# Both w transforms of a spectral layer as four 64x64 tiles, with the residual kept on chip in rows split by parity

## The chip, the cores and the metric

The kernel runs on one core of one Trainium2 chip. The metric is the device time of one execution in microseconds. The kernel before takes 3664.48 us, the median of 3 runs (3661.27 to 3665.77).

## The reference

The input x has shape (2, 48, 48, 768): two images of 48 by 48 tokens and 768 channels, all in f32. Two layers follow each other, both with a residual:

```
x = x + attention(group_norm(x))        # 12 heads of 64, relative positions in h and w, then proj_w, proj_b
x = x + spectral(group_norm(x))

spectral(v):
    f = rfft2(v, axes=(h, w), norm="ortho")           # 48 x 25 complex per channel
    o1 = gelu(complex block matmul(f, w1) + b1)       # 8 blocks of 96 channels
    o2 = softshrink(complex block matmul(o1, w2) + b2, 0.01)
    return irfft2(o2, s=(48, 48), norm="ortho")
```

The change concerns the end of the first layer (projection and residual) and the two one-dimensional transforms over w in the second: the forward one at the beginning, the inverse one at the end.

## The kernel before, in words

**Stages.** The attention of both images comes first. Then, for each image b, `project_out` (L887) multiplies the attention's output by proj_w, adds it to x, and takes the transform over w; `Spectral` (L952) does the rest of layer 1. While one stage ends, steps of the next projection are run ahead of time: `Projection.fill` and `step` (L811 to L818) are called from attention and from `prepare` in `block_kernel` (L1270).

**The order of the work.** The kernel is written in Bass and Tile; a pool of tiles hands out memory and inserts the waits. Instructions through `InOrder` (L60) stay on their engine in the order in which the program issues them; its line, L68, is the one that the profile gives them. Each engine works through its queue in order. SP (SyncE) issues nearly all DMAs. A DMA of the program takes one of eight completion semaphores in turn, so that it waits for the one eight before it.

**Attention's last steps.** `finish` (L553) copies the output of a unit (18 units for each pair of heads; three share one `res` tile) and stores each full `res` to `oT` in DRAM; `inverses` (L571) transposes the reciprocal denominators on PE (`ps_i`), copies them (`turned`) and stores them to `inv_d` with three DMAs, one for each of three columns x. The last of these end attention.

**The projection.** NT = 18 token tiles of 128 tokens, each in two channel halves of UQ = 384 columns. `Projection.tokens` (L859) loads, for a group g of three token tiles, `oT` and the reciprocals and multiplies them on POOL. `Projection.product` (L843) accumulates six matmuls, 128x128 by 128x384, into a PSUM bank `acc`. PSUM has eight banks, of which this part uses seven.

`project_out` keeps x, and then x1 = x + attention, in six tiles `x2` of 96 rows (two image rows of 48 tokens) by XP = 4 row pairs by 768 channels. `rows(i)` (L900) loads one of them, and POOL adds the bias proj_b to it in four instructions. For each product, `shifts` (L746) cuts the 128 tokens into pieces that lie on aligned partitions, 3 for each token tile, and DVE adds them into `x2` (L941). When four image rows are complete, and one more token tile is under way, `over_w(g)` (L912) transforms them: four matmuls with `fw` (96 rows by 112 columns, block diagonal for two image rows), each over 384 columns, into banks `ps_y`, four copies by ACT (L927) into `y1`, and one store of `y1` by SP to `y_d`, 112 rows. There are 12 such over_w in an image. After the last token tile the over_w still left are done by channel halves.

**The spectral layer.** It goes through four sections s of SC = 192 channels (two blocks n each). `load` (L1079) reads `y_d` into `y2` in five pieces; `over_h` (L1089) transforms over h (`ps_z`); `mean`, `norm`, `first` and `second` (L1040 to L1186) do the group norm and the MLP; `back_h` (L1188) transforms back over h and stores `u_d`. `back_w(s, more)` (L1204) does for one section the inverse transform over w and the residual: for each of the six tiles of `x2`, two matmuls with `iw` (100 rows by 96 columns, 384 columns of `u2`) into `ps_x`, two DVE adds into `x2` (L1221), the fetch of the next section's `u2` (100 rows by 4 row pairs), and the store of the section's channels to `out`. `run` (L1233) calls it with the fetches of the next section one section ahead, and at the end `prepare(True)` and a last `back_w`.

**Between the two images.** In the last section of image A, `prepare` gets the second image's projection ready: memory, weights, the first tokens and the first multiply. The fourier constants `fh`, `fw`, `ih`, `iw`, `gmean` are loaded anew for each image, after `rows(0)`.

Of the kernel before, what the change touches and what calls it, by code (L numbers as in the profile page):

```python
# [17 lines left out]
P = 128  # L18
# [24 lines left out]
YP = 112  # L43
# [232 lines left out]
def attention(tc, k, xs, a, oTs, inv_ds, late, span, ps_b, ps_o):  # L276
# [12 lines left out]
    with ExitStack() as ctx:  # L289
# [63 lines left out]
        by_act, by_dve = [], []  # L353

# [197 lines left out]

        def finish(un):  # L553

            pr, g, x = un["pr"], un["g"], un["x"]
            if x == 0:
                outs[pr, g] = outp.tile([P, 8, 3, 16], F32, tag="res", name="res")
                if g % 3 == 0:
                    dens[pr, g // 3] = outp.tile([P, 3, 2, 3], F32, tag="dens", name="dens")
            res = outs[pr, g]  # L560
            act.copy(res[:, :, x, :], un["o"][:, :P].rearrange("p (y d) -> p y d", d=16))
            dve.tensor_reduce(
                dens[pr, g // 3][:, x, :, g % 3], un["parts"], AX.X, ALU.add
            )
            if x == 2:
                sync.dma_start(
                    out=oTs[pr // NP][pr % NP * P : (pr % NP + 1) * P, g * UQ : (g + 1) * UQ],
                    in_=res.rearrange("p y x d -> p (y x d)"),
                )

        def inverses(pr, half):  # L571
# [12 lines left out]
            def send():  # L584
                dst = inv_ds[pr // NP][pr % NP, half].rearrange("h g (y x d) -> x (h g) y d", x=3, d=16)
                for x in range(3):
                    sync.dma_start(
                        out=dst[x],
                        in_=turned[6 * x : 6 * x + 6, :].rearrange("p (y d) -> p y d", d=16),
                    )  # L590
# [3 lines left out]
        pairs = NP * xs.shape[0]  # L594
# [151 lines left out]
def shifts(t):  # L746


    size = {0: P, 32: 32, 64: 64, 96: 32}
    p = 0  # L750
    while p < P:
        hp, q = divmod(t * P + p, 2 * HW)
        n = min(P - p, 2 * HW - q, size[p], size[q])
        yield p, hp, q, n
        p += n


class Projection:
# [27 lines left out]
    def cut(self, whole, i):  # L786

        return whole[:, self.head + i * NCC * UQ :][:, : NCC * UQ]
# [10 lines left out]
    def w(self):  # L799
        return self.fixed()[:, : NCC * C].rearrange("p (cc f) -> p cc f", f=C)  # L800

    @property
    def pb(self):
        return self.fixed()[:, NCC * C : self.head]
# [82 lines left out]
def project_out(tc, k, x_b, pr, pools, y_d, x2, constants):  # L887
# [9 lines left out]
    R = 2 * HW  # L897
    x_v = x_b.rearrange("(t p) c -> p t c", p=R)

    def rows(i):  # L900

        part = x2[i]
        pr.sync.dma_start(out=part, in_=x_v[:, i * XP : (i + 1) * XP, :])
        for j in range(XP):
            pr.pool.tensor_tensor(part[:, j, :], part[:, j, :], pr.pb[:R], ALU.add)

# [3 lines left out]
    row = lambda hp: x2[hp // XP][:, hp % XP, :]  # L910

    def over_w(g, steps=range(C // SC)):  # L912

        y1 = work.tile([YP, 2, C], F32, tag="y1", name="y1")
        part = x2[2 * g // XP]
        t0 = 2 * g % XP
        for s in steps:
            ch = slice(s * SC, (s + 1) * SC)
            ps = bank("ps_y")
            nc.tensor.matmul(  # L920
                ps[:YP, : 2 * SC],
                lhsT=k.fw,
                rhs=part[:, t0 : t0 + 2, ch],
                start=True,
                stop=True,
            )
            nc.scalar.copy(y1[:, :, ch], ps[:YP, : 2 * SC].rearrange("p (t c) -> p t c", c=SC))  # L927
        ch = slice(steps[0] * SC, (steps[-1] + 1) * SC)
        pr.sync.dma_start(out=y_d[:, 2 * g : 2 * g + 2, ch], in_=y1[:, :, ch])

    turned = 0
    for t in range(NT):
        if t % 3 == 0 and 0 < t < NT - 3:
            pr.tokens(t // 3 + 1)
            rows(t // 3 + 1)
        for hf in range(2):
            cols = slice(hf * UQ, (hf + 1) * UQ)
            acc = pr.product(t, hf)
            for p, hp, q, n in shifts(t):
                dst = row(hp)[q : q + n, cols]  # L940
                nc.vector.tensor_tensor(dst, acc[p : p + n, :UQ], dst, ALU.add)  # L941
            if t == NT - 1:
                half = C // SC // 2
                for g in range(turned, HW // 4):
                    over_w(g, range(hf * half, (hf + 1) * half))
        while t < NT - 1 and (turned + 1) * 2 * R <= (t - 1) * P:
            over_w(turned)
            turned += 1
# [3 lines left out]
class Spectral:  # L952
# [12 lines left out]
    def __init__(self, tc, k, a, pools, x2, y_d, out_b, prepare):  # L965
        self.tc, self.nc, self.k, self.a, self.prepare = tc, tc.nc, k, a, prepare
        self.sync = InOrder(tc, tc.nc.sync)
        self.span, self.ps_b, self.small, self.wp, self.yp, self.up, self.dp, zp = pools
        self.x2, self.y_d = x2, y_d
        self.out_v = out_b.rearrange("(t p) c -> p t c", p=2 * HW)  # L970
# [21 lines left out]
        self.y2, self.u2, self.w, self.power = {}, {}, {}, {}  # L992

# [56 lines left out]
    def norm(self, n):  # L1050
# [24 lines left out]
        for f0 in range(0, NF, 400):  # L1075
            fs = slice(f0, f0 + 400)
            nc.gpsimd.tensor_tensor(self.both[n % 2][:, fs], zf[:, 0, fs], zf[:, 1, fs], ALU.add)

    def load(self, s, pieces):  # L1079

        src = self.y_d[: 4 * KW, :, s * SC : (s + 1) * SC].rearrange(
# [7 lines left out]
    def over_h(self, n):  # L1089
# [7 lines left out]
        for j in range(KW // WP):  # L1097
# [13 lines left out]
            if n == 1 and j == 1:  # L1111
                self.mean(0)
            if n == 1 and j == 3:
# [30 lines left out]
    def second(self, n, ahead):  # L1144
# [9 lines left out]
        for j in range(KW // WP):  # L1154
# [22 lines left out]
            nc.gpsimd.tensor_tensor(val, val, clip, ALU.subtract)  # L1177
# [25 lines left out]

    def back_w(self, s, more):  # L1204


        nc, k = self.nc, self.k
        ch = slice(s * SC, (s + 1) * SC)
        u_d = self.u_d.rearrange("w (q t) c -> (w q) t c", q=4)
        for i, part in enumerate(self.x2):  # L1210
            for t in range(0, XP, 2) if s >= 0 else ():
                ps = self.bank("ps_x")
                nc.tensor.matmul(  # L1213
                    ps[: 2 * HW, : 2 * SC],
                    lhsT=k.iw,
                    rhs=self.u2[s, i][:, t : t + 2, :],
                    start=True,
                    stop=True,
                )
                dst = part[:, t : t + 2, ch]  # L1220
                nc.vector.tensor_tensor(  # L1221
                    dst, ps[: 2 * HW, : 2 * SC].rearrange("p (t c) -> p t c", c=SC), dst, ALU.add
                )
            if more:
                u2 = self.up.tile([4 * KW, XP, SC], F32, tag="u2", name="u2")
                self.sync.dma_start(out=u2, in_=u_d[:, i * XP : (i + 1) * XP, :])
                self.u2[s + 1, i] = u2
            if s >= 0:
                self.sync.dma_start(
                    out=self.out_v[:, i * XP : (i + 1) * XP, ch], in_=part[:, :, ch]  # L1230
                )
# [38 lines left out]
def block_kernel(tc, a, out):  # L1270
    nc = tc.nc
    B = a["x"].shape[0]
    with ExitStack() as ctx:
# [21 lines left out]
        for b in range(B):  # L1295
            oTs.append(dram.tile([C, S], F32, tag=f"oT{b}", name=f"oT{b}"))
            y_ds.append(dram.tile([YP, HW // 2, C], F32, tag=f"y_d{b}", name=f"y_d{b}"))
# [13 lines left out]
        def prepare(rest):  # L1311
# [9 lines left out]
            while rest and ready[-1].steps:  # L1321
                ready[-1].step()

        attention(tc, k, a["x"], a, oTs, inv_ds, late, span, ps_b, ps_o)
        for b in range(B):
            with ExitStack() as ctx2:
# [3 lines left out]
                x2 = [  # L1330
                    pool(f"x2_{i}", 1).tile([2 * HW, XP, C], F32, tag="x2", name=f"x2_{i}")
                    for i in range(HW // 2 // XP)
                ]
# [113 lines left out]
```

## Time and profile before

The profiled execution took 3660.19 us and its span is 3658.4 us; the runs shown have a median of 3664.48 us. PE's granted clock has a mean of 0.987. All times in the table are of that execution, in us from the start of the span.

| what | value |
|---|---|
| time of the profiled execution | 3660.19 us |
| span | 3658.4 us |
| PE busy | 3548.6 us (97%) |
| DVE, ACT, POOL busy | 79%, 70%, 56% |
| attention of both images | 0 to 2838 |
| projection and forward w transform, image A | 2838 to 2988 |
| rest of layer 1, image A | 2988 to 3236 |
| projection and forward w transform, image B | 3236 to 3406 |
| rest of layer 1, image B | 3406 to 3658 |
| ps_y (L920) | 192 records on PE, 66.8 us busy after 2838 |
| ps_x (L1213) | 192 records on PE, 66.7 us busy |
| adds of the product on DVE (L941) | 216, 553 ns each |
| adds of the inverse transform on DVE (L1221) | 96, 553 ns each |
| copies of ps_y on ACT (L927) | 96, 479 ns each |

How to read it: PE is the TensorE's matmuls, PEld its weight loads. An f32 matmul leaves two records (two passes), so a count of records is twice the count of matmuls. DVE is VectorE, ACT ScalarE, POOL GpSimd; SPq is SyncE's queue, where a DMA is issued. `out<-in` names the tiles written and read. The chain of waits is followed back from the last instruction: at each step to what released it. Idle time of an engine that is not the bottleneck costs nothing.

### The profile page before, as it was taken

Reading aid. Unit: us, or ns where it says so; the run is one execution under the profiler, and the core shown is the slowest. Engines: PE = TensorE matmul, PEld = TensorE weight load, DVE = VectorE, ACT = ScalarE, POOL = GpSimd, SP = SyncE. Lnnn points to the kernel's source line nnn. Section 1 sums busy time; section 2 is a strip of 40 time slices with the busy share of each in tenths; the row PEclk is TensorE's granted clock in tenths of the full one; section 3 lists DMA queues with packets and bytes.
Section 4 is the critical chain, followed back from the end, with each engine's and each line's share of the span. In section 5 each row is a group of like instructions: output and inputs, shape, how many; then the busy total and the mean of one; then the engine's idle time right before and its main releaser. Section 6 shows DMA issues by size and latency. Waiting matters only on the chain.

```text
span 3658.4 us, 92606 instructions
## 1 busy us (share of the span) xinstructions
PE 3548.6 (97%) x36032; PEld 2477.2 (68%) x36032; DVE 2902.1 (79%) x6771; ACT 2557.2 (70%) x3769; POOL 2047.2 (56%) x662
## 2 busy tenths in 40 slices
PE   7999999999999999999999999999988999999898
PEld 5677676767767666677676767767666557655675
DVE  4798989989989996799898989899996437743576
ACT  3788888888888888688888888888885124301342
POOL 2567666757575763567666666666673524343232
PEclk9999999999999999999999999999999989999999
DMA  3687778777777885677777777777888743585434
GB/s 105 142 181 171 180 171 179 172 179 171 181 169 175 214 200 122 140 178 174 176 176 171 177 173 175 176 176 172 188 190 190 200 127 85 169 213 147 109 110 140
DMA packets 496484, 607.61 MB, mean 166 GB/s; under 512 B 179117, under 2 KB 311597, under 8 KB 496046
## 3 DMA queue, kind: packets, MB, share of 16 engines
q1 hardware_dynamic: 496046, 601.68, 69.3%
q8 instruction: 286, 4.69, 0.6%
q14 instruction: 152, 1.25, 0.1%
HBM read 131.60 MB, written 87.67 MB: 60 GB/s over the span
## 4 chain that ended last, share of the span: by engine, by line
PE 84%; DVE 5%; ACT 3%; DMA 3%; issue 2%; POOL 1%; SPq 1%; POOLq 0%; DVEq 0%; ACTq 0%
PE ps_o L68 22%; PE ps_s L68 21%; PE ps_proj L68 15%; PE ps_v L68 8%; PE acc L68 7%; DVE s L68 2%; PE ps_u L1195 2%; PE ps L1160 2%; PE ps_y L920 2%; PE ps_r L68 2%; SPq L68 1%; PE ps_x L1213 1%; DMA pT<-s 1%; ACT spectrum L1035 1%; POOL s L68 1%
## 5 line engine op out<-in xcount | busy, mean ns | idle before, releaser
L68 POOL TENSOR_TENSOR s<-rhw 128x2304 f32<-128x2304 f32 x432 | 1740.8, 4062 | 1025.3 <-DMA pT<-s 546.8
L68 DVE CUSTOM_DVE_ANT_0 s<-ps_s,s 128x512 f32<-128x512 f32 (+1 forms) x2160 | 1222.2, 633 | 299.7 <-issue 196.1
L68 ACT ACTIVATE s<-s,nm 128x1152 f32<-128x1152 f32 x864 | 1074.7, 1245 | 335.3 <-DVE nm L68 333.1
L68 DVE STREAM_TRANSPOSE s<-s 128x1152 f32<-128x1152 f32 x864 | 1112.0, 1344 | 6.8 <-ACT s L68 6.8
L68 ACT COPY pT<-s 32x1152 f32<-32x1152 f32 x864 | 993.6, 1150 | 25.9 <-PE ps_o L68 7.5
L68 PE MATMUL ps_o<-pT,v 128*64 128x128 f32 x15552 | 906.5, 276 | 41.7 <-ACT res L68 18.9
L68 PEld LDWEIGHTS ps_o<-pT,v 128*64 128x64 f32 x15552 | 875.4, 139 | 84.0 <-issue 43.6
L68 PE MATMUL ps_s<-kT,qT 64*128 64x512 f32 (+1 forms) x4320 | 899.8, 554 | 4.9 <-DVE mx L68 1.7
L68 PEld LDWEIGHTS ps_s<-kT,qT 64*128 64x128 f32 x4320 | 432.3, 186 | 418.1 <-issue 347.0
L68 PE MATMUL ps_proj<-xnT,w 128*64 128x384 f32 (+1 forms) x4032 | 591.3, 446 | 4.9 <-ACT xnT L68 3.7
L68 PEld LDWEIGHTS ps_proj<-xnT,w 128*64 128x64 f32 x4032 | 281.0, 137 | 278.8 <-issue 212.1
L941 DVE TENSOR_TENSOR x<-acc,x 32x384 f32<-32x384 f32 (+2 forms) x216 | 119.2, 553 | 227.8 <-PE acc L68 163.8
L68 PE MATMUL ps_v<-w,xnT 128*64 128x128 f32 x5184 | 297.3, 274 | 0.0
L68 PEld LDWEIGHTS ps_v<-w,xnT 128*64 128x64 f32 x5184 | 281.7, 137 | 21.2 <-DVE mx L68 21.2
L927 ACT COPY y<-ps_y 112x384 f32<-112x384 f32 x96 | 46.0, 479 | 299.5 <-PE ps_y L920 282.7
L68 DVE DVE_READ_ACCUMULATOR2_ANT mx<- 128x1 f32 x2160 | 179.7, 83 | 0.0
L68 ACT ACTIVATION_READ_ACCUMULATOR s<-s,nm 128x1 f32 x864 | 161.4, 187 | 0.0
L1177 POOL TENSOR_TENSOR spectrum<-spectrum 128x480 f32<-128x480 f32 x80 | 96.3, 1204 | 113.2 <-DVE spectrum L1176 85.0
L1160 PE MATMUL ps<-w,spectrum 96*64 96x96 f32 x3200 | 143.1, 248 | 0.0
L1160 PEld LDWEIGHTS ps<-w,spectrum 96*64 96x64 f32 x3200 | 133.6, 137 | 11.1 <-issue 4.4
L68 PE MATMUL acc<-proj_s 128*128 128x384 f32 x360 | 118.2, 486 | 0.4 <-POOL x L68 0.4
L68 PEld LDWEIGHTS acc<-proj_s 128*128 128x128 f32 x360 | 68.3, 190 | 48.2 <-POOL x L68 0.6
(139 smaller groups left out, 2299.8 us busy)
## 6 DMA issues: line engine op xcount, KB each, us to landing
pT<-s SPq DMA_DIRECT2D x2592, 144.0 KB
t<-rel SPq DMA_DIRECT2D x144, 189.0 KB
rhw<-t SPq DMA_DIRECT2D x144, 144.0 KB
y<-y_d SPq DMA_DIRECT2D x40, 360.0 KB
u_d<-spectrum SPq DMA_DIRECT2D x40, 360.0 KB
u<-u_d SPq DMA_DIRECT2D x48, 300.0 KB
w<-in_qkv_w SPq DMA_DIRECT2D x36, 384.0 KB
oT<-res SPq DMA_DIRECT2D x72, 192.0 KB
```

What stands on the lines that cost most here:

```text
L68: return lambda *args, **kw: self.tc.keep_in_program_order(op(*args, **kw))
L920: nc.tensor.matmul(ps[:YP, : 2 * SC], lhsT=k.fw, rhs=part[:, t0 : t0 + 2, ch], start=True, stop=True,)
L927: nc.scalar.copy(y1[:, :, ch], ps[:YP, : 2 * SC].rearrange("p (t c) -> p t c", c=SC))
L941: nc.vector.tensor_tensor(dst, acc[p : p + n, :UQ], dst, ALU.add)
L1035: self.nc.scalar.activation(junk, part, AF.Square, accum_out=total)
L1160: nc.tensor.matmul(ps[64 * r : 64 * r + 64, w * BS : (w + 1) * BS], lhsT=self.o1[:, ri, f0 : f0 + 64], rhs=w2[:, (0, 2, 1, 0)[2 * r + ri], ...
L1177: nc.gpsimd.tensor_tensor(val, val, clip, ALU.subtract)
L1195: nc.tensor.matmul(ps[: 2 * HW, :480], lhsT=k.ih, rhs=d2[:, c0 : c0 + 480], start=True, stop=True)
L1213: nc.tensor.matmul(ps[: 2 * HW, : 2 * SC], lhsT=k.iw, rhs=self.u2[s, i][:, t : t + 2, :], start=True, stop=True,)
```

## The change

In words:

- The residual is one tile `x1` of 128 partitions by 24 row pairs by 768 channels, held over both images and put at a place that attention's memory occupied. Even image rows lie on partitions 0 to 47, odd ones on 64 to 95 and 112 to 127 (tokens 0 to 31 and 32 to 47 of the row). Partitions 48 to 63 and 96 to 111 are filled with other rows and meet zeros in `fw`. A group of rows is loaded by four or five DMAs (it was one), and `moves` cuts a token tile into 3, 5 and 5 pieces for the adds (it was 3 each).
- `over_w` uses `fw` as 64x64 tiles: for each channel half four matmuls, one for each combination of two row groups and two column groups, into two banks, with one ACT copy for each bank. `y1` is stored by two DMAs of 50 rows, issued by ACT.
- over_w(2g) stands right after token tile 3g+2, and over_w(2g-1) after token tile 3g: one token tile sooner than before. The last three token tiles go by channel halves: all of half 0, then all of half 1, with the over_w in between.
- `back_w` uses `iw` in the same way: 24 matmuls of 50 rows by 64 columns instead of 12 of 100 by 96. `u2` is fetched by two DMAs of 50 rows. The stores to `out` are three for each three groups of rows (18 in the last section), and the fetches are no longer each followed by a store.
- In attention `inv_d` is stored by five DMAs instead of three, in an order that makes parities contiguous; for the last unit these and the store of `oT` are issued by ACT.
- `prepare` also runs two products (`fill(2)`) for the second image before its `back_w`. The fourier constants are loaded once. `mean(0)` and `norm(0)` come one piece of over_h sooner. The pool of `y2` has 10 buffers (it had 8). POOL's instructions of the spectral layer go through `InOrder`.

```diff
 def finish(un):  def send():
+        def queue(pr, g):
+            return act if (pr, g) == (pairs - 1, HW // 8 - 1) else sync
...
                 for x in range(3):
-                    sync.dma_start(
-                        out=dst[x],
-                        in_=turned[6 * x : 6 * x + 6, :].rearrange("p (y d) -> p y d", d=16),
-                    )
+                    src = turned[6 * x : 6 * x + 6, :].rearrange("p (k i d) -> p k i d", i=2, d=16)
+                    if x == 2:
+                        to.dma_start(
+                            out=dst[:, :, 1, :], in_=src.rearrange("p k i d -> p k (i d)")
+                        )
+                        continue
+                    for i in range(2):
+                        to.dma_start(
+                            out=dst[:, :, 2 * i, 16 * x : 16 * x + 16], in_=src[:, :, i, :]
+                        )
...
+def moves(t):
+    done = 0
+    for p in range(0, P, 32):
+        k, m = divmod(t % 3 * 4 + p // 32, 3)
+        if p >= done:
+            n = min(P, p + 96 - 32 * m) - p if p in (0, 64) and m == 0 else 32
+            yield p, n, k, 32 * m
+            done = p + n
+        if m == 1:
+            yield p, 32, k, 96
...
+    def rows(g):
+        part = x1[:, 4 * g : 4 * g + 4, :]
+        pr.sync.dma_start(out=part[:HW], in_=x_v[g, 0])
+        pr.sync.dma_start(out=part[64:96], in_=x_v[g, 1, :32])
+        for i in range(2):
+            pr.sync.dma_start(out=part[96 + 16 * i : 112 + 16 * i], in_=x_v[g, i, 32:])
+        if pr.room is None:
+            pr.sync.dma_start(out=part[HW:64], in_=x_v[g, 1, 32:])
+        for j in range(4):
+            pr.pool.tensor_tensor(part[:, j, :], part[:, j, :], pr.pb, ALU.add)
...
+    def over_w(n, halves=range(2)):
+        y1 = work.tile([P, 2, C], F32, tag="y1", name="y1")
+        for hf in halves:
+            cols = slice(hf * UQ, (hf + 1) * UQ)
+            both = [bank(f"ps_y{i}") for i in range(2)]
+            for c in range(2):
+                for i in range(2):
+                    r = slice(64 * i, 64 * i + 64)
+                    pr.pe.matmul(
+                        both[i][64 * c : 64 * c + 64, :UQ],
+                        lhsT=k.fw[r, :],
+                        rhs=x1[r, 2 * n + c, cols],
+                        start=True,
+                        stop=True,
+                        skip_group_check=True,
+                    )
+            for i in range(2):
+                nc.scalar.copy(y1[:, i, cols], both[i][:, :UQ])
+        cols = slice(halves[0] * UQ, (halves[-1] + 1) * UQ)
+        for c in range(2):
+            nc.scalar.dma_start(
+                out=y_v[2 * n + c, :, :, cols], in_=y1[64 * c : 64 * c + 2 * KW, :, cols]
             )
...
+    for t in range(NT - 3):
+        g = t // 3
+        if t % 3 == 0 and t:
+            pr.tokens(g + 1)
+            rows(g + 1)
         for hf in range(2):
+            outputs(t, hf)
+        if t % 3 == 2:
+            over_w(2 * g)
+        elif t % 3 == 0 and g:
+            over_w(2 * g - 1)
+    c = HW // 4 - 1
+    for hf in range(2):
+        for t in range(NT - 3, NT):
+            outputs(t, hf)
+            if t == NT - 3:
+                if hf:
+                    over_w(c, (0,))
+                else:
+                    over_w(c - 2)
+        over_w(c - 1, (hf,))
+    over_w(c, (1,))
...
     def back_w(self, s, more):
...
+        for j in range(parts):
+            if s >= 0:
+                both = [self.bank(f"ps_x{m}") for m in range(2)]
+                for i in range(2):
+                    for m in range(2):
+                        r = slice(64 * m, 64 * m + 2 * KW)
+                        pe.matmul(
+                            both[m][64 * i : 64 * i + 64, : 2 * SC],
+                            lhsT=k.iw[r, i, :],
+                            rhs=self.u2[s, j][r, i],
...
+                for m in range(2):
+                    dst = self.x1[:, j * XP + 2 * m : j * XP + 2 * m + 2, ch]
+                    self.nc.vector.tensor_tensor(
+                        dst, both[m][:, : 2 * SC].rearrange("p (t c) -> p t c", c=SC), dst, ALU.add
+                    )
             if more:
+                self.fetch(s + 1, j)
+            if s >= 0 and (j + 1) % each == 0:
+                ts = slice((j + 1 - each) * XP, (j + 1) * XP)
+                for q, i, w0, n in ((0, 0, 0, HW), (64, 1, 0, 32), (112, 1, 32, 16)):
+                    self.sync.dma_start(
+                        out=self.out_v[i, w0 : w0 + n, ts, ch], in_=self.x1[q : q + n, ts, ch]
+                    )
...
             while rest and ready[-1].steps:
                 ready[-1].step()
+            if rest and not ready[-1].accs:
+                ready[-1].fill(2)
```

## The prediction

> **What bounds the kernel now.** I read the page first: PE is busy 97% of the span and holds 84% of the chain that ended last, so time is gained by shorter PE work or by filling PE's gaps. The projections and spectral stages lie after 2838 us. There I followed the chain of waits, in order of time (start, length, engine, tile, line):
>
> ```profile
> 2716.07 4.07 PE ps_s L68 x20
> 2720.14 4.02 PE ps_proj L68 x24
> 2724.36 4.08 PE ps_o L68 x72
> ...
> 2830.91 7.13 POOL x L68 x4
> 2838.15 7.98 PE acc L68 x24
> 2846.12 2.58 PE ps_y L920 x8
> 2848.71 7.74 PE acc L68 x24
> 2856.45 2.58 PE ps_y L920 x8
> 2859.03 15.48 PE acc L68 x48
> ...
> 2972.58 3.88 PE acc L68 x12
> 2978.89 1.51 PE ps_y L920 x4
> 2980.40 3.89 PE acc L68 x12
> 2986.71 1.53 PE ps_y L920 x4
> 2989.11 5.27 DMA y<-y_d
> 2994.52 6.56 PE ps_z L1100 x40
> ...
> 3117.91 7.74 PE ps_x L1213 x24
> ...
> 3219.96 3.97 DMA u<-u_d
> ...
> 3236.47 30.96 PE acc L68 x96
> 3267.43 2.58 PE ps_y L920 x8
> ```
>
> The reader sees both projections as a column of PE pieces, 7.74 us for one token tile and 2.58 us for one over_w (eight records: four f32 matmuls, two passes each), each starting where the last one ended. The holes are at the end: 2972.58 + 3.88 is 2976.46, but ps_y starts at 2978.89; then the load of y (5.27) stands alone. What releases the projection's start is x: POOL adds the bias to it up to 2838.04.
>
> The table by windows says the same of the stage (length, then busy PE, PEld, DVE, ACT, POOL; clock; DMA share; GB/s):
>
> ```profile
> 2838.00:2988.00 150.00, 147.56 (x456) 85.06 (x456) 55.22 (x100) 22.38 (x48) 59.28 (x34) 1.00 0.66 167
> 3393.00:3416.00 23.00, 16.36 (x63) 9.24 (x61) 5.11 (x10) 6.66 (x16) 0.12 (x1) 0.97 0.60 159
> ```
>
> PE works 147.56 of 150 us, then 16.36 of 23 at the tail of image B. SyncE's queue at the first start is the last view:
>
> ```profile
> 2818.30 0.56 SPq L68 DMA_DIRECT2D x<-in_x  x1
> 2837.84 0.34 SPq L68 DMA_DIRECT2D oT<-res  x1
> 2838.28 2.40 SPq L68 DMA_DIRECT2D inv_d<-turned  x3
> ```
>
> x is asked for 20 us before attention's last store.
>
> **The quadrant matmul.** over_w's four 96x112 matmuls become, in each half, four of 64x64, two per PSUM bank, still 384 columns and two passes. A pass of 384 columns is 7.74/24 = 0.32 us. The trace has no 64x64 row, so I bound it by pairs. The 20 records of ps_s (64-row tiles: 16 of 512 columns, 4 of 256) would take 16 x 0.43 + 4 x 0.215 = 7.7 us one by one and take 4.07; the 72 of ps_o (64-column tiles, 128 columns) would take 7.7 and take 4.08. Two tiles run at once in either direction. If the four quadrants only pair, an over_w stays 16 x 0.32 / 2 = 2.58 us: gain zero. If all four run together it is 1.29. Between: in the records, ps_s starts both first passes 6 ns apart and both second passes 0.43 us later, while ps_o alternates 103 and 6 ns, as if a second pass were issued before the neighbour's first. With both habits the row pair goes together and the column pair follows a pass later, so one pass (0.32) is added at the start: 1.29 + 0.32 = 1.6 us. I take 1.6, nearest to both rows, gain 0.98 each; twelve per image.
>
> Three rows above, ps_s, ps_proj and ps_o change the tiling twice, with 0.00 and 0.20 us between them. The Trainium skill ("TensorEngine Tiling (Array Packing)", Key Properties) says that a change of tiling mode drains TensorE, which speaks against 64x64 work between full-array products; at the 0.20 just seen, two changes in each of 24 over_w would be at most 10 us, at the 0.00 nothing.
>
> back_w goes the same way, 7.74 us to about 4.6 at best. But its twelve DVE adds (553 ns each, some 0.60 apart with DVE as the pace) need 7.2 us. With seven banks PE may run ahead by that many, so what it wins is what the next PE work can use without DVE: after the first of an image next to nothing (0.6, ps_z is copied by DVE and ACT), after the second about 2 us, after the third nothing, since the load of u (3.97 above) ends that wait. The last is paced by loads of u and stores of out. Norm and mean come one piece earlier, 1.3 us. Together **-4 us per image**, between 0 and -8, and -0.5 at the kernel's end (two loads of 50 rows for one of 100 carry the same bytes).
>
> **Image A's start.** All of x1 is now one tile, and it overlays memory that attention still uses. In the changed program the first x load waits for the last stores of inv_d, moved with oT to ScalarE's queue behind the copies that end at 2838.0. Three stores took 2.40 us to issue; five take 4.0, so 2842, and a completion of 2 to 3 us gives 2845. The load is five DMAs of 1.57 MB: 6.4 us at the 246 GB/s that the windows show for 3633 to 3658, 9.4 at this stage's 167; the inv_d load before it took 8.03. I say 7: landed at **2852**, where before it was there at 2830. POOL's adds are 7.12/4 = 1.78 us, so rows j=0..3 are ready at 2853.8, 2855.6, 2857.3, 2859.1. DVE adds follow at 0.55; over_w(0) needs j=0,1 with t=0,1 added in both halves, about 2862. PE cannot jump it: the order is written out, and it now stands before token tile 3. Six products filled earlier hide nothing, as they are done at 2838. Then 7.74 + 1.6 + 7.74 gives 2880 for five token tiles and two over_w, where the chain shows 2859.03: **21 us lost**, bounds 8 (POOL and DVE alone after 2840) and 30 (a load at half rate).
>
> Queued behind the waiting x load on SP are the second x load and tokens; POOL waits with it. Constants and weights go ahead of it and are no one's wait.
>
> From there 13 tiles x 7.74 = 100.6 and 10 over_w. Before: 100.6 + 25.8 from 2859.03 is 2985.5, and ps_z goes on at 2994.5, so the tail held 9 us of holes. Now the outputs go by channel halves: half 0 of the last three tiles is stored some 10 us before the end, so the loads of y for the first blocks are covered, and only the last over_w waits for DVE adds, 2.3 us. 2880 + 100.6 + 16 + 2.3 = 2999. All of ps_z for block 0 is still to do then, 2 us more than before. So image A's projection is 2999 - 2994.5 + 2 = **+6**, bounds -8 and +16.
>
> **Image B's start.** Before: 3236.47 to 3280.34 for the same five tiles and two over_w, x landing near 3258 behind stores of out. Now two products are filled during the wait for u, but only four more cover x, and that load is 1.34 MB for 1.15 in the same crowded stretch; POOL and DVE as above give 3286: +6, bounds 0 and +12. Ten over_w give -9.8; the tail's idle (12.9 us of PE work after 3393.88 ended at 3416.1, so 9.3) shrinks to 2.3: -7. Sum **-11**, bounds -20 and 0.
>
> **Side costs.** The adds of the product go from 108 to 156 an image, 48 x 0.553 = 27 us more DVE; in a stage where DVE worked 55 of 150 us this hides under PE (13 us of adds per 26 us of tiles). If a group's x came late it would show at once. The stores of y on ACT's queue are two issues of some 0.5 us; ACT worked 22 of 150. In attention 48 more stores of inv_d, 0.8 us each, sit on SP under a PE that is 97% busy: +1.5 us, bounds 0 and 3.
>
> The y store before was one of 112 rows; now two of 50. Under the Trainium skill ("DMA: Bandwidth & Descriptors", Why a DMA increments its semaphore by 16 and not by 1) the number of engines is the largest up to 16 that divides the rows: 16 before, 10 now, so by the page a store moves at 10/16 of the rate; no row here shows it.
>
> **Sum** against the profiled execution, 3660.19: 1.5 + 6 - 4 - 11 - 4 - 0.5 = -12, so 3648. That execution lies 4.3 us under the median of the runs shown (3664.48); the same -12 from the median gives **3652**.
>
> **Rivals.** (1) *Quadrants only pair.* Four tiles through one in-order queue issue pass after pass; the 103 and 6 ns of ps_o are what that looks like. Then the change does not do what it says: over_w 2.58, back_w 7.74. Twenty over_w give back 19.6, back_w 5: 3652 + 25 = 3677. For it: no row of four. Against: ps_s pairs its first passes. (2) *The start takes the place of the tail, on the slower side.* The first x load behind the inv_d stores is the one mechanism: each us that it lands after 2852 is a us at the end, and from 2864 on the change is slower. With the load at half the stage's rate, 19 us, it lands at 2864, and image B with it 8 later: 3652 + 12 + 8 = 3672. For it: the busy stage, 0.66 DMA share. Against: 2838 to 2850 has no exchange of p left. (3) *Better than forecast*: 1.29 per over_w (-6), x landed at 2845 (-7), no loss at B's start (-6), back_w in full (-3): 3630. (4) DVE becomes the pace: 13 of 26 us speak against it; inside the range.
>
> **How the numbers follow.** Forecast 0.50, own range 3644 to 3661; of it 0.42 is faster by over 0.2% and 0.08 within (0.2%, or 7.3 us, is about what a measurement of this kernel can tell from no change). Rival 1: 0.20; rival 2: 0.12; rival 3: 0.14; mixtures near no change: 0.04. So faster 0.42 + 0.14 = 0.56, same 0.12, slower 0.32. The range goes from rival 3 with a little more (3626) to rivals 1 and 2 (3682).
>
> **What would show it.** ps_y as x16 in 1.3, 1.6 or 2.6 us on the chain; PE idle from 2838 to some 2860 with x<-in_x issued near 2845; ps_z following ps_y without a load of y between; DVE's adds never releasing PE outside the first and last groups; ps_x at 4.6 to 7 us. It is wrong if ps_y stays at 2.58, if x lands before 2842 (then near 3640), or if the later groups of x rows also hold PE.

## The result, and the profile after

The changed kernel takes 3689.88 us (median of 4 runs, 3688.56 to 3692.71) against 3664.36 before: a ratio of 1.0072, 95% interval 1.0054 to 1.0089. The forecast was 3652. Its profiled execution took 3690.66 us with a span of 3688.9.

PE's starts and ends in the timeline cut both executions into the same stretches. "To last ps_y" means from the mark before it; a mark is the end of the last piece of its kind in that image (for ps_1r the start of the first).

| stretch, us | before | after | moved by | forecast |
|---|---|---|---|---|
| attention, to last ps_o | 2837.5 | 2842.9 | +5.4 | +1.5 |
| image A: to last ps_y | 150.7 | 171.1 | +20.4 | |
| to first ps_1r | 23.4 | 18.9 | -4.5 | +6 with the line above |
| to last ps_u | 202.6 | 196.8 | -5.8 | |
| to last ps_x | 22.2 | 24.5 | +2.3 | -4 with the line above |
| image B: to last ps_y | 173.1 | 179.2 | +6.1 | |
| to first ps_1r | 21.9 | 22.5 | +0.6 | -11 with the line above |
| to last ps_u | 201.7 | 196.9 | -4.8 | -4 |
| to last ps_x | 20.4 | 24.2 | +3.8 | |
| to the end | 4.9 | 11.8 | +6.9 | -0.5 with the line above |

The chain of waits of the changed kernel shows image A's start, its steady part and its tail:

```profile
2838.82 4.11 PE ps_o L67 x72
2843.93 1.33 ACTq L67
2847.63 2.04 DMA inv_d<-turned
2851.53 11.10 DMA x<-in_x
2862.79 3.57 POOL x L67 x2
2869.37 5.47 PE ps_y L67 x12
2874.84 9.93 PE acc L67 x24
2884.77 1.45 PE ps_y L67 x16
2886.22 15.68 PE acc L67 x48
2901.90 1.45 PE ps_y L67 x16
2903.35 7.94 PE acc L67 x24
...
2996.58 0.81 PE ps_y L67 x8
2997.39 4.07 PE acc L67 x12
3001.45 0.93 PE ps_y L67 x8
...
3139.53 4.20 PE ps_x L67 x48
...
3272.19 12.37 issue
3285.09 3.57 POOL x L67 x2
3291.68 4.81 PE ps_y L67 x12
3296.49 7.94 PE acc L67 x24
...
3435.45 8.79 PE ps_z L1144 x50
...
3666.52 4.23 DMA u<-u_d
3670.89 6.22 PE ps_x L67 x24
```

The reader sees the cheap over_w, 1.45 us where 2.58 stood, and ps_x in 4.20 where 7.74 stood. Before them stands a new piece, the load of x (11.10; the first of its five DMAs is issued at 2849.75, right after the last store of inv_d has landed, 2847.63 + 2.04), and then POOL, DVE and PE one after another until 2874.84: 32 us from the last ps_o to the first product behind over_w(0). At 3272.19 the same hole stands in image B ("issue" there is the transfer of x, which the chain doesn't name). SP's queue (start, length, what, how many) and the table by windows (columns as before) say when x was asked for and how fast it came:

```profile
2833.38 12.27 SPq L1057 DMA_DIRECT2D b<-in_b  x2
2845.70 1.95 SPq L1068 DMA_DIRECT2D w<-in_w  x3
2849.75 11.70 SPq L67 DMA_DIRECT2D x<-in_x  x10
```
```profile
2856.00:2863.00 7.00, 0.00 (x0) 0.00 (x0) 0.00 (x0) 0.00 (x0) 0.21 (x1) 0.50 1.05 144
2863.00:2870.00 7.00, 3.71 (x5) 0.85 (x6) 4.61 (x9) 0.00 (x0) 6.87 (x4) 0.50 1.04 153
```

The same window view of the kernel before, while later x loads of image A run beside loads of oT and inv_d:

```profile
2846.00:2851.00 5.00, 5.00 (x17) 2.90 (x16) 0.00 (x0) 1.92 (x4) 0.24 (x1) 1.00 1.05 249
```

The DMA engines are as busy in both (1.05), but move 144 to 153 GB/s after and 249 before. PE's granted clock is 0.50 in the hole, and the first token tile behind it (24 records) takes 9.93 us instead of 7.74.

### The profile page after: what moved, and what is told of

Read it like the earlier page. It is cut to its first block, busy times and chain, and to the rows that moved or that the text cites. A ratio compares the mean times of both kernels' runs of the same rounds, so it can differ in the third digit from the quotient of the medians.

```text
span 3688.9 us, 93785 instructions
## 1 busy us (share of the span) xinstructions
PE 3528.8 (96%) x36416; PEld 2445.3 (66%) x36416; DVE 2940.0 (80%) x6867; ACT 2550.6 (69%) x3769; POOL 2045.4 (55%) x662
## 4 chain that ended last, share of the span: by engine, by line
PE 84%; DMA 5%; DVE 3%; SPq 2%; ACT 2%; POOL 2%; issue 2%; ACTq 0%; DVEq 0%; POOLq 0%
PE ps_o L67 21%; PE ps_s L67 20%; PE ps_proj L67 15%; PE ps_v L67 8%; PE acc L67 7%; PE ps L1204 3%; SPq L67 2%; DVE s L67 2%; PE ps_r L67 2%; PE ps_z L1144 2%; DMA pT<-s 1%; PE ps_y L67 1%; PE ps_u L1239 1%; PE ps L1179 1%; PE ps_1r L1179 1%
## 5 line engine op out<-in xcount | busy, mean ns | idle before, releaser
L67 PE MATMUL ps_o<-pT,v 128*64 128x128 f32 x15552 | 902.9, 276 | 49.9 <-DMA pT<-s 21.6
L968 DVE TENSOR_TENSOR x<-acc,x 32x384 f32<-32x384 f32 (+2 forms) x312 | 173.0, 554 | 201.6 <-POOL x L67 108.2
L955 ACT COPY y<-ps_y 128x384 f32<-128x384 f32 x96 | 40.0, 490 | 333.9 <-PE ps_y L67 332.1
L67 DVE DVE_READ_ACCUMULATOR2_ANT mx<- 128x1 f32 x2160 | 179.2, 83 | 0.0
```

The costliest lines, as they stand in the source:

```text
L67: return lambda *args, **kw: self.tc.keep_in_program_order(op(*args, **kw))
L955: nc.scalar.copy(y1[:, i, cols], both[i][:, :UQ])
```

## The experiments

Theory 1 at the start: the stores of out (18 instead of 6 in the last section) cost time on SP's queue at the end of both images, and the x load is late in image A because it waits for memory. Theory 2: bytes and a slow x load. Six marks, in us, for the profiled execution of each run (first ps_y is its start, A counted from the last ps_o, B from the last ps_x of image A):

| run | first ps_y A | first ps_y B | first ps_1r A, B after last ps_y | last ps_u to last ps_x, B | last ps_x to end |
|---|---|---|---|---|---|
| before | 8.5 | 30.8 | 23.4, 21.9 | 20.4 | 4.9 |
| after | 22.3 | 33.3 | 18.9, 22.5 | 24.2 | 11.8 |
| e1_six_stores | 22.8 | 29.1 | 19.2, 23.0 | 24.5 | 12.2 |
| e1b_act_stores | 22.5 | 28.6 | 23.2, 23.8 | 27.4 | 10.3 |
| e2_six_tiles | 10.0 | 30.3 | 17.6, 22.8 | 28.8 | 9.1 |
| e5_before_18_stores | 8.5 | 33.1 | 23.6, 25.7 | 20.4 | 7.0 |
| e6_before_5_inv | 8.5 | 32.4 | 20.7, 25.3 | 20.2 | 5.0 |
| e7_before_unmixed | 8.5 | 31.0 | 20.5, 22.4 | 22.8 | 4.4 |
| e8_after_mixed | 22.6 | 31.7 | 18.2, 22.4 | 23.0 | 12.9 |
| e9_x_on_act | 22.4 | 29.3 | 18.1, 18.8 | 23.5 | 12.1 |
| e10_before_narrow | 20.2 | 32.4 | 19.8, 25.0 | 20.0 | 9.7 |
| e11_before_wide | 8.5 | 30.8 | 20.7, 25.2 | 20.5 | 7.4 |
| e16_narrow_but_first | 8.5 | 33.3 | 23.0, 25.5 | 20.0 | 9.4 |
| e12_before_halves | 8.5 | 30.8 | 14.7, 24.6 | 20.7 | 4.9 |
| e15_halves_act | 8.5 | 32.6 | 14.7, 22.8 | 20.3 | 4.9 |
| e13_x_in_three | 21.6 | 27.6 | 19.0, 23.6 | 24.7 | 11.7 |
| e14_no_x_load | 9.0 | 20.3 | 19.5, 23.3 | 24.7 | 11.3 |

In the kernel before, PE works through one token tile (image A) and four (image B) ahead of the first ps_y; in the changed kernel through none and two, and the rest of the time it is idle. So these two columns compare runs of the same kernel; between the kernels the sums further down count. Each row is one execution. Rows whose edit doesn't touch a stretch show how far one profile goes: the way to the first ps_1r scatters from 20.5 to 23.6 in image A and from 21.9 to 25.7 in image B (before, e5, e6, e7), the first ps_y of image B from 30.8 to 32.6 (before, e6, e12, e15), the last two columns by 0.5 and 0.1 (before, e6, e12, e15).

**How many stores.** The changed kernel with fewer, with some on another queue, and the kernel before with more:

```diff
# e1_six_stores, on the changed kernel
-        each = 1 if s == NBK // NB - 1 else parts // 2
+        each = parts // 2
# e1b_act_stores, on the changed kernel
-                    self.sync.dma_start(
+                    (act if each == 1 and q else self.sync).dma_start(
# e5_before_18_stores, on the kernel before: one store of out in the last section becomes three
+                cut = (0, 48, 80, 96) if s == NBK // NB - 1 else (0, 96)
```

> The changed kernel, but the last section stores out in 6 pieces (three for each half of the rows) instead of 18; the other sections already did. Theory 1 (the extra stores cost time on SP's queue, 0.65 to 0.87 us for each issue): 12 fewer issues in front of image B's first x load and 12 fewer at the kernel's end, so 6 to 10 us less at each place and 3670 to 3677 in all against 3690. Theory 2 (the bytes and the slow x load are what limits there, whatever the number of stores): the bytes are the same, so within 4 us of 3690. Against theory 1 speaks that the stores of a half now start later, after three groups instead of one.

> The changed kernel, but in the last section the 12 stores of odd image rows are issued on ScalarE's queue, the 6 of even rows stay on SP. Theory 1 (SP's queue): as far as six stores, or further, since no store starts later: 3668 to 3676, and the end after the last ps_x falls from 11.8 us to 5 to 7. Theory 2 (bytes): 3686 to 3692.

> The kernel before, with nothing of the change but one thing: each store of out in the last section is cut into three by partitions (48, 32, 16), 18 instead of 6. Theory 1 (SP's queue): 12 more issues at 0.65 to 0.87 us ahead of image B's x load and at the end: 3664 becomes 3676 to 3684. Theory 2 (bytes): 3664 within 4.

e1: 3687.92 us, ratio to before 1.0063 (1.0048 to 1.0078). Image B's first ps_y comes 4.2 sooner, the way from the last ps_x to the end is not shorter. e1b: 3705.43 in its one run, worse nearly everywhere behind attention; why stays open. e5: 3668.14, 1.0009 (0.9999 to 1.0019), of which the profile shows 2.1 at the end and 2.3 at image B's start. Theory 1 fails in size: the number of stores is worth 2 at the end of the kernel before, nothing at that of the changed one, and 2 to 4 at image B's start, not 6 to 10. What the stores do there stands in SP's queue, of the kernel before, the changed one and e1:

```profile
3232.62 14.51 SPq L68 DMA_DIRECT2D out<-x  x6
3248.27 0.33 SPq L68 DMA_DIRECT2D x<-in_x  x1
```
```profile
3256.48 15.72 SPq L67 DMA_DIRECT2D out<-x  x18
3272.24 10.06 SPq L67 DMA_DIRECT2D x<-in_x  x8
```
```profile
3255.75 9.49 SPq L67 DMA_DIRECT2D out<-x  x6
3266.32 11.10 SPq L67 DMA_DIRECT2D x<-in_x  x8
```

Counted from the last ps_x of image A, the x load is issued at 11.8, 18.0 and 12.7, and POOL starts on it at 21.6, 30.8 and 26.6. So the later issue behind 18 stores is part of image B's loss, and the longer transfer (12.8 and 13.9 from issue to POOL, where it was 9.8) is another.

**The wait for memory.** x1 as six tiles, the first where the kernel before had its own:

```diff
+        x1 = [ctx.enter_context(tc.tile_pool(name=f"sp_x{i}", bufs=1)).tile([P, XP, C], F32,
+              tag="x1", name=f"x1_{i}") for i in range(HW // 2 // XP)]
-        part = x1[:, 4 * g : 4 * g + 4, :]
+        part = x1[g]
```

> The changed kernel, but x1 is six tiles in six pools, the first of which lies where the kernel before had its first x tile; for that every section stores out in 18 pieces (the last one did already). Theory 1 (the x load is late because it waits for attention's last stores): the first x load is issued near 2823, lands before 2845, and PE's hole of 26 us after attention shrinks to some 5; image A's first five token tiles end near 2870 instead of 2894, so 3665 to 3671 against 3690. Theory 2 (the x load is slow by itself, 1.57 MB at 150 GB/s, and the following groups then hold PE): the hole moves from the first group to the second, 3680 to 3690. The extra stores of sections 0 to 2 should be hidden, or cost up to 5 us in all.

3682.50 us, 1.0048 (1.0033 to 1.0063). The first part of the x load is issued at 2824.21 and POOL starts on it at 2850.68: early enough to take 12.3 from the first ps_y, but 7.5 us after the last ps_o all the same, since the last two of its five parts still wait for attention's last store of oT, which lands at 2845.36. Section ends are longer (28.8, every section now has 18 stores). The theory holds for half of image A's hole.

**The order of fetches and stores, and the queue.**

```diff
# e7_before_unmixed: after every third fetch, the three stores
-            if s >= 0:
+            if s >= 0 and i % 3 == 2:
+                for h in range(i - 2, i + 1):
# e8_after_mixed: e1, and one pending store after each fetch
                 self.fetch(s + 1, j)
+                if pend:
+                    pend.pop(0)()
# e9_x_on_act: e1, and image B's first two x loads on ScalarE's queue
+        q = InOrder(tc, nc.scalar) if pr.room is not None and g < 2 else pr.sync
```

> The kernel before, with one thing of the change: in back_w the fetches of u and the stores of out are no longer one for one; three fetches, then the three stores that belong to them, and again. Numbers and sizes stay. Theory 3 (a fetch of u alone keeps only 10 of 16 DMA engines at work, as the packets after 3670 show with 9 to 11 at a time, and needs the stores beside it to come to 15): the way from the last ps_u to the end, 25.3 us before, grows by 4 to 8, image B's x load comes 3 to 6 later, 3664 becomes 3671 to 3678. Theory 4 (the size of the pieces, two fetches of 50 rows for one of 100, makes it slow; the order does nothing): 3664 within 3.

> The changed kernel with six stores in the last section, and the stores of the first three groups issued one by one between the fetches of the last three. Theory 3 (order): the way from the last ps_u to the end, 36.7 us with six stores, falls to 31 to 33, image B starts 2 to 4 sooner: 3678 to 3683. Theory 4 (pieces): within 3 of the 3688 with six stores alone.

> The changed kernel with six stores in the last section, and image B's first two x loads issued on ScalarE's queue instead of SP's. If x is late there because it is issued behind the stores and the tokens on SP (at 3266 with six stores), it is issued some 5 to 10 us sooner and the first ps_y of image B comes 4 to 8 sooner than 3282.7; if the DMA engines are what x waits for, it lands as before, within 2.

e7: 3663.46, 1.0004 (0.9994 to 1.0013). e8: 3688.39, 1.0067 (1.0052 to 1.0082). Theory 3, the order, falls. e9: 3683.79 in one run; x was issued at 3268.28, no sooner than on SP in e1 (3266.32): in both chains a store of out lands just before it (3268.21 and 3266.25), so the load waits on either queue.

**The stores of inv_d**, five instead of three, in the kernel before:

```diff
+                    for i in range(2 if x < 2 else 1):
+                        ys = slice(4 * i, 4 * i + 4) if x < 2 else slice(0, 8)
+                        sync.dma_start(out=dst[x][:, ys, :], in_=src[:, ys, :])
```

> The kernel before with one thing of the change: inv_d is stored by five DMAs instead of three, through SP. If these stores make attention's end later by 5.4 us in the changed kernel, the last ps_o ends at 2841 to 2844 here; if it is something else (the constants and weights on SP, the changed res copies), at 2837 to 2839.

3666.22 in one run; the last ps_o ends at 2838.5, 1.0 later than in the kernel before. Since it ends anywhere from 2836.9 to 2838.7 in e5, e7, e11, e12 and e15, which leave these stores alone, that they cost anything is not shown.

**Narrow against wide.** The kernel before with equal counts, bytes and order, cut by partitions or along the row pairs:

```diff
# e10_before_narrow
+        for q0, q1 in ((0, 48), (48, 80), (80, 96)):
+            pr.sync.dma_start(out=part[q0:q1], in_=x_v[q0:q1, i * XP : (i + 1) * XP, :])
# e11_before_wide
+        for j0, j1 in ((0, 2), (2, 3), (3, 4)):
+            pr.sync.dma_start(out=part[:, j0:j1], in_=x_v[:, i * XP + j0 : i * XP + j1, :])
# both: u in two fetches, the last section's out in three stores, cut likewise
# e16_narrow_but_first: e10, with image A's first load whole
+        cuts = ((0, 48), (48, 80), (80, 96)) if i or pr.room is not None else ((0, 96),)
```

> The kernel before, its layout and order, but with transfers cut by partitions as the change has them: each x load in three (48, 32, 16 rows), each fetch of u in two (50 and 50), the last section's stores of out in three. Theory 5 (a transfer that touches few partitions moves its packets slower): packets of 3072 bytes of x in the projection take 280 to 340 ns instead of 203 to 221, image A's first ps_y comes no later (x is loaded early there), but image B's does, by 4 to 8, and the way from the last ps_u to the end grows from 25 to 31 or more: 3672 to 3684. Theory 6 (only the count of DMAs costs): the same time as its twin, cut across all partitions. Theory 7 (the early x load and the 36% more bytes are all): 3664 to 3668.

> The twin: the kernel before with exactly as many DMAs, each cut along the row pairs, so that each still touches all 96 or 100 partitions (x in 2+1+1 row pairs, u in 2+2, the last stores in 2+1+1). Theory 5: packets of x stay at 200 to 225 ns, 3663 to 3670. Theory 6: the same time as the one cut by partitions, 3670 to 3684.

> The kernel before with the transfers cut by partitions as in the narrow run, but the very first x load of image A whole. In the narrow run the second and third part of that load came to stand behind attention's last stores (issued at 2843, the first at 2821), which is the order of the queue and not the width. If that was most of its 14 us, 3664 to 3672 here; if the slower packets of narrow transfers cost the time themselves, 3674 to 3680.

e10: 3678.80, 1.0042 (1.0028 to 1.0055). e11: 3664.24, 1.0004 (0.9995 to 1.0013). e16: 3669.61, 1.0018 (1.0009 to 1.0027). In the trace's DMA packets from the last ps_o to the last ps_y of image A, the 3072-byte packets (nearly all of them x) take 204 ns on average in e11 and 215 before, but 268 in e10 and 264 in e16: cut by partitions, a packet takes some 30% longer than in the twin, while the count alone costs nothing measurable. SP's queue shows why e10 lost 12 us more at image A's start, first of e10 and then of e11:

```profile
2820.97 0.50 SPq L68 DMA_DIRECT2D x<-in_x  x1
2840.41 0.34 SPq L68 DMA_DIRECT2D oT<-res  x1
2840.86 2.38 SPq L68 DMA_DIRECT2D inv_d<-turned  x3
2843.28 0.92 SPq L68 DMA_DIRECT2D x<-in_x  x2
```
```profile
2818.02 1.87 SPq L68 DMA_DIRECT2D x<-in_x  x3
2837.47 0.35 SPq L68 DMA_DIRECT2D oT<-res  x1
```

Two of its three parts stand behind attention's last stores. e16 takes that away (8.5 again), and what width costs then is 0.2%.

**Fewer x DMAs, and none** (in e14 POOL writes twice the bias instead, so the residual of the first two groups of rows in each image is not x).

```diff
# e13_x_in_three: e1, and for image A
+            pr.sync.dma_start(out=part[:64], in_=x_w[g, :64])
+            pr.sync.dma_start(out=part[64:112], in_=x_v[g, 1])
+        pr.sync.dma_start(out=part[112:], in_=x_v[g, 1, 32:])
# e14_no_x_load
+        if g < 2:
+            for j in range(4):
+                pr.pool.tensor_tensor(part[:, j, :], pr.pb, pr.pb, ALU.add)
+            return
```

> The changed kernel with six stores in the last section and each x load in three DMAs: in image A 64, 48 and 16 rows (the rows that meet zeros in fw get other tokens of x, so no byte less), in image B 48, 32 and 16 (14% fewer bytes). Theory 5: image A's first ps_y comes 2 to 4 sooner than 22.8 after attention (64 and 48 rows at a time are wider than 48, 32, 16, 16, 16), image B's 1 to 2 sooner. Theory 6: 1.5 sooner (two issues less). Theory 7: 0 and 1.

> The changed kernel with the x loads of the first two groups of each image left out: POOL writes twice the bias there in the same instructions, so the residual of those rows is not x. What is left of the hole after attention is then the wait for memory and POOL, DVE and PE in turn; what goes is the transfer. If the transfer is the dear part (13 us from issue to POOL in image A), image A's first ps_y comes 9 to 13 us sooner than 22.3 after attention, and image B's needs no load behind the stores, 14 to 18 sooner than 33.3 after the last ps_x: 3660 to 3668. If the memory that attention still holds is what counts, image A gains under 5 and the time stays over 3672.

e13: 3687.78 in one run, 1.2 and 1.5 sooner at the two starts than e1. e14: 3665.93 in one run. PE's timeline of e14 at image B, and then of the changed kernel:

```profile
3242.24 17.74 PE L67 MATMUL acc<-proj 128*128 128x384 f32 x48
3262.59 0.83 PE L67 MATMUL ps_y<-x,fw 64*64 64x384 f32 x2 [2.61 <-DVE x L972]
```
```profile
3254.18 17.47 PE L67 MATMUL acc<-proj 128*128 128x384 f32 x48
3287.58 1.51 PE L67 MATMUL ps_y<-x,fw 64*64 64x384 f32 x2 [15.92 <-DVE x L968]
```

The idle time in brackets falls from 15.92 to 2.61; image A's first ps_y comes 13.3 sooner, image B's 13.0. POOL still waits there for what the load had to wait for: attention's last inv_d store until 2852.96, 6.6 after that run's last ps_o, and a store of out until 3260.34, 18.0 after the last ps_x. So what goes is the transfer alone. Without these loads the kernel takes 24 us less, nearly as much as the whole change lost.

**What of the change gains alone.** The kernel before with the last three token tiles by channel halves and the earlier norm (e12), and with y stored on ScalarE's queue too (e15):

```diff
+    outputs(NT - 1, 0)
+    over_w(c - 1, halves[0])
+    outputs(NT - 3, 1)
+    over_w(c, halves[0])
+    outputs(NT - 2, 1)
+    outputs(NT - 1, 1)
+    over_w(c - 1, halves[1])
+    over_w(c, halves[1])
-            if n == 1 and j == 1:
+            if n == 1 and j == 0:
```

> The kernel before with only the two parts of the change that the profile after shows to gain: the last three token tiles by channel halves (with the over_w between them), and mean(0) and norm(0) one piece earlier. Layout, matmuls and loads are those of before. If the tail's holes close as in the changed kernel (its way from the last ps_y to ps_1r is 18.9 against 23.4, and ps_y never waits for more than 0.3 there), image A and B gain 4 to 8 each: 3648 to 3656. If the gain hung on the smaller over_w, which leave DVE time, 3660 to 3664.

> The kernel before with the last three token tiles by channel halves and the earlier norm, as in the run before, and the stores of y on ScalarE's queue. There image A's tail fell from 23.4 to 14.7 us, but image B's did not (24.5), and the trace shows three of its five loads of y standing on SP behind the two last stores. On another queue the loads stand behind no store: image B gains 5 to 9 more, 3645 to 3650. If it is the DMA engines that hold these loads, 3652 to 3656.

e12: 3654.14 us, 0.9972 (0.9962 to 0.9983), faster than both kernels. e15: 3652.74, 0.9971 (0.9961 to 0.9982), no better than e12. PE's timeline of e12 at image A's tail:

```profile
2974.93 1.46 PE L68 MATMUL ps_y<-x,fw 96*112 96x384 f32 x4
2976.22 7.91 PE L68 MATMUL acc<-proj_s 128*128 128x384 f32 x24
2983.96 1.46 PE L68 MATMUL ps_y<-x,fw 96*112 96x384 f32 x4
2986.56 1.52 PE L68 MATMUL ps_y<-x,fw 96*112 96x384 f32 x4 [1.14 <-DVE x L937]
2987.91 5.26 PE L1115 MATMUL ps_z<-fh,y 96*96 96x96 f32 x60
```

ps_z follows ps_y with no load between. In image B no gain is seen there (24.6 and 22.8 against a scatter of 21.9 to 25.7), and a queue of its own for the stores didn't bring it. In e15 PE's clock falls to 0.50 there (0.60 from 3400 to 3410, 0.50 to 3420), and the loads of y run at a DMA share of 1.12; which of these holds it was not separated.

## Why the prediction was wrong, point by point

Against its own terms the forecast was 9 us too low at image A's start, 10 at image B's, 8 in image B's tail, 11 at the kernel's end and 4 in attention.

- **Over_w, the price right, the picture not.** 1.6 us was forecast and 1.45 came. All four first passes start within 20 ns and the four second passes 0.37 us (then 0.32) later, so four tiles do run at once; the forecast had the second pair a pass later. Each token tile behind an over_w takes 7.94 instead of 7.74, so 0.2 is given back and the net is 1.65: that it met the 1.6 is in part luck. The Trainium skill ("TensorEngine Tiling (Array Packing)", Key Properties: changing the mode drains TensorE) agrees in kind; the measured price is 0.2 us for each over_w, 5 us in all, half of the 10 that were put as its bound. Rival 1 (only pairs) is dead.
- **back_w and norm, right in sum.** 4.20 against 4.6 at best; image A -5.8 to the last ps_u and +2.3 to the last ps_x, so -3.5 against -4, and image B -4.8. The parts were not right: the norm's 1.3 falls before the first ps_1r, and e12, which has it without the new back_w, is no shorter from there to the last ps_u (203.1 and 201.9). So -5.8 and -4.8 stand against 2.6 for back_w; POOL's new order falls in the same stretch, and the two were not separated.
- **Image A's steady part and tail, right.** From five token tiles and two over_w (2859.0 and 2894.1) to ps_1r the time fell by 13.8; the forecast's own terms gave 15.
- **Image A's start, the step that failed first: "I say 7: landed at 2852".** The wait was the right one: x is issued when the last inv_d store has landed, and the biases and weights ahead of it, issued by 2847.65, were no one's wait. But it was issued at 2849.75, not 2845: the copies ahead of the stores end at 2843.9, not 2838.0, as attention ended later; the five stores (3.7) and the landing (2.0) were as forecast. The load landed at 2862.6, 13 us later and not 7. The forecast took a rate between 167 and 246 GB/s from stretches with other transfers; this one has 144 to 153. Of the 8.7 by which the loss, counted from attention's end, came out higher (29.7, not 21), the transfer is 6; 2.2 is the first token tile at the lower clock. That it waits at all was right: e2 takes 12 away by asking earlier.
- **Image B's start, the same step in a crowded stretch: "+6".** From the last ps_x of image A to five token tiles and two over_w it is 59.4 us against 43.9, so +15.5, nearly all of it the hole of 15.92 shown above. POOL and DVE were counted, the transfer only as in the kernel before, and its turn behind 18 stores not at all. x is issued 6.2 later and then takes 3.0 longer to reach POOL; the kernel before had four token tiles to cover it, this one two. e14, without the transfer, takes 13.0 away; e1, with six stores, 4.2; e9 shows that the queue was not it.
- **Image B's tail: -17 for over_w and tail, measured -8.8.** The early half of y was there (PE waits 1.0 us for y), but PE went through ps_z at a granted clock of 0.50 (3436 to 3456), with DMA share over 1.0: the 100 records of ps_z take 16.8 us, where image A's took 11.1. Why the clock fell there, with under 2 us of idle time on PE just before, stays open.
- **The kernel's end: -0.5, measured +10.7.** "Carry the same bytes" was true and beside the point. Of the 10.7, 6.9 lie behind the last ps_x: three stores for one explain 2 to 3 (e5, e11), cutting them and the fetch by partitions 2 more (e10, e16); the rest was not separated. PE's clock is 0.50 to 0.52 there after 3660, and the last ps_x take 6.2 us for 24 records where 48 took 4.2.
- **Attention: +1.5, measured +5.4.** That the stores of inv_d are part of it is not shown (e6). In e1, e1b, e8, e9, e13 and e14, whose attention is that of the changed kernel, the last ps_o ends at 2841.0 to 2846.4. In the profile shown most of the 5.4 arises between 2615 and 2800, where first_o and first_inv are loaded between the exchanges of p; its cause stays open.

Of the rivals, the second (the start takes the place of the tail) named the mechanism and the place; its price of 20 over the forecast was too low, as the kernel's end wasn't in it.

An estimate of the transfer's factor: 1.57 MB at 150 GB/s is 10.5 us, 1.18 MB (the 1152 KB of a load before) at 249 is 4.7. The bytes are 1.33 of the 2.2; slower packets are the rest, 1.66, of which the twin shows 1.3 for 48, 32 and 16 rows. That pieces of 16 rows are slower still was not tried. The load also had company: of the 628 packets of 3072 bytes that start between its issue and its landing, it needs 512, and the other 116 belong to the second group, issued right behind it. They take 312 ns on average, against 213 in the window of the kernel before; 628 of them over 16 engines are 12.2 us, the 512 alone 10.0.

## What to carry to other kernels

Price a load by the partitions that each DMA touches, not only by bytes and count: a layout that suits PE's tiles is paid for at every transfer into it, and that price stands on the path wherever nothing else covers the load. Before a new order takes cover away from a load, do the sum for that load by itself. When a change bundles several edits, try the ones that need no new layout alone: here they were the faster kernel.

## What the hardware showed

- Transfers of 3072-byte packets cut by partitions took 264 to 268 ns for each packet against 204 for the wide twin. The Trainium skill ("DMA: Bandwidth & Descriptors", The descriptor swizzle) says that a transfer over 128 partitions spreads its writes over all SBUF ports, with partitions 0 to 63 on even and 64 to 127 on odd ones. By that, 48 rows from partition 0 would reach half of the ports, which may be the reason; no run here shows ports.
- In a hole of 22 us on PE the granted clock fell to 0.50 (0.50 from 2850 to 2870), and the first token tile after it took 9.93 us instead of 7.74, at a mean clock of 0.80.
- The same DMA share can mean 144 or 249 GB/s, so a share alone doesn't say that a transfer is done well.
